# A CIN layer stack on one core: the shared terms V1 and V0 as matmuls of 32 by 64, with x loaded in halves for them

## The chip, the cores and the metric

The kernel runs on one core of a Trainium2 chip. The metric is the device time of one execution in microseconds (us), lower is better. The time before is 486.74 us, the median of 3 runs (486.42 to 490.46). All data is float32.

## What is computed

A compressed interaction network with three layers over x of shape (B = 1024, F = 64, E = 16), cut to what matters:

```python
for i in range(3):
    z = jnp.einsum('bfe,bge->bfge', x0, h).reshape(B, 64 * 64, 16)   # all products of x0 and h
    y = jnp.einsum('oc,bce->boe', Ws[i], z) + bs[i][None, :, None]   # 128 outputs
    x_i, h = (y[:, :64], y[:, 64:]) if i != 2 else (y, y)            # first half kept, second half goes on
    xs.append(x_i)
pooled = jnp.sum(jnp.concatenate(xs, axis=1), axis=2)
return pooled @ fc_w.T + fc_b
```

The result is one number for each of the 1024 rows. Because what is kept of a layer is only summed with the weights of `fc_w`, the kept half of layer 0 is a quadratic form of x (its 64x64 matrix is called V0 here), the kept half of layer 1 is x times V1 times h1, and layer 2 is a quadratic form too, whose matrix (V2, W2 weighed with `fc_w`) is folded into weights called Q. Only the half of layer 0 that goes on, h1, needs all 64 outputs.

## The kernel before, in words

The host sorts x into 32 chunks of 32 rows: a chunk is 64 features by N = 512 columns (32 rows times E). For each chunk the kernel loads `xa` (128 partitions x 4 x 512, x shifted by 0 to 3 features) and `xb` (128 x 4 x 512, x shifted by more), 1 MB each, from SP's queue (`load_xa`, `load_xb`, lines 131 to 148). `xra` holds 132 rows of 512 for each chunk, and the first 64 of them are x itself.

Work for one chunk:

- `product` (line 219): VectorE multiplies `xa` by `xb` for j = 0 to 3, 128 x 2048 each, into tiles `z` (12 buffers). After the last one ScalarE writes a 32-row square into z (line 228).
- `contract` (line 256): 16 matmuls of 128x128 by 512 columns for each chunk, accumulated in PSUM (`acc`): one half of the rows is h1, the other half is Q's part (which half depends on whether the chunk is odd).
- `contract_shared` (line 265), once for four chunks: V1 times x is added to the Q half (line 274), V0 times x goes to tiles `ys` (line 278), and the squares of x's first 32 features times `w_sq` are added to `acc` (line 284). For V1 and V0 two chunks stand above each other in a tile `xx` (128 x 512), and each matmul takes 64 rows and 64 columns of the array. The weights are `v1w` and the diagonal blocks of `bd`. For the squares four chunks stand in one tile `sq`, 32 rows each, and each matmul takes 32 rows and 64 columns.
- `squares` (line 230) and `last_tile` (line 236): ScalarE makes `sq` from `xa` (32 rows at a time, line 234) and copies x from `xa` into `xx` (64 rows at a time, line 243).
- `factors` (line 324): ScalarE copies the Q half out (line 330), and VectorE adds the bias to h1 and multiplies the two (line 336). `x_v0x` (line 340): VectorE multiplies `ys` by `xx`. `sums` (line 343): VectorE sums over E.

Stages. A head (to some 43 us) loads weights and four chunks (2, 3, 0, 1), computes h1 for them with matmuls of 128x64 by 256 (line 296), makes V2 and from it Q (through a DRAM tile `md` and back, lines 450 to 533), and then adds Q's part for chunks 0 and 1 (`head_q`, line 310, matmuls of 128x64 by 512). Then the main loop goes through the chunks in the order 4, 5, 6, 7, 2 and 3 (head chunks), 8, 9, and so on to 31. Loads and products run ahead of the matmuls by two chunks, as buffers come free (3 buffers for `xa`, 3 for `xb`).

The order of work is written out by hand: each engine runs its instructions in the order of the program, and so does SP with the transfers that it issues. Ahead of the main loop the order on VectorE is: products of chunk 4; `w1x` is weighed with `fc_w` (`weigh`, lines 570 and 571) into `v1h`, which four copies of 64x32 put into `v1w` (line 582); products of chunk 5. Within the loop's first step: `w0x` is weighed, and four copies put `v0h` into `bd` (line 594); products of chunks 6 and 7. SP issues in the same order: chunk 4, `w1x`, chunk 5, `w0x`, chunk 6, chunk 7. `keep_clock` (line 103) lets TensorE run some matmuls with a cleared `bd` at the very start.

Of the kernel before, what the change touches and what calls it, by code (L numbers as in the profile page):

```python
# [33 lines left out]
F32 = mybir.dt.float32  # L37
AF = mybir.ActivationFunctionType
# [3 lines left out]
F = 64  # L42
E = 16
B = 1024
CB = 32
N = CB * E
# [5 lines left out]
XR = 128 + NI  # L52
# [3 lines left out]
KEPT = HEAD[-2:]  # L56
NV = 200
FIRST = 4
# [4 lines left out]
def cin_kernel(ctx, tc, xra, xrb, wh, w0r, w1h, w2t, wx1, wx0, vec, out):  # L63
    nc = tc.nc
# [17 lines left out]
    def flat_tile(name):  # L82
        return z_tile(name).rearrange("p i n -> p (i n)")
# [11 lines left out]
    fv2 = const_tile("fv2", [128, 32])  # L95
    nc.scalar.copy(fv2, fc2.to_broadcast([128, 32]))

    bd = const_tile("bd", [128, 128])
    nc.gpsimd.memset(bd, 0.0)

    misc = ps.tile([128, N], F32, tag="acc", name="misc", bufs=4)

    def keep_clock(n):
        for _ in range(n):
            nc.tensor.matmul(misc[:, 0:128], bd, bd, start=True, stop=True)  # L105

    keep_clock(6)

    shift = const_tile("shift", [128, 96])
    nc.gpsimd.memset(shift, 0.0)  # L110
    for base in (0, 64, -64):
        nc.gpsimd.affine_select(
            out=shift, in_=shift, compare_op=ALU.not_equal, fill=1.0, base=base,
# [9 lines left out]

    w_all = const_tile("w_all", [128, NT, 192])
    w_sq = const_tile("w_sq", [128, 192])
    v1w = const_tile("v1w", [128, F])


    xas, xbs, xxs, sqs = {}, {}, {}, {}

    def load_xa(c, at=slice(0, NI)):
        if c not in xas or at.start == 0:
# [9 lines left out]
    def load_xb(c, first=NJ):  # L142

        xb = xp.tile([128, NJ, N], F32, tag="xb", name=f"xb_{c}")
        for at in (slice(0, first), slice(first, NJ)):
            if at.start < NJ:
                nc.sync.dma_start(out=xb[:, at, :], in_=xrb[c, :, at, :])
        xbs[c] = [xb[:, j, :] for j in range(NJ)]

    def load_chunk(c):  # L150
        load_xa(c)
        load_xb(c)

    c0, c1, c2, c3 = HEAD
# [51 lines left out]
    accs, uus, zs, ys, parts = {}, {}, {}, {}, {}  # L206
# [20 lines left out]
        if j == NJ - 1:  # L227
            nc.scalar.activation(zs[c, j][SQ, 0, :], xas[c][SQ, 0, :], AF.Square)  # L228

    def squares(c):  # L230
        if c // 4 not in sqs:
            sqs[c // 4] = xp.tile([128, N], F32, tag="zl", name=f"sq_{c}", bufs=3)
        at = slice(32 * (c % 4), 32 * (c % 4) + 32)
        nc.scalar.activation(sqs[c // 4][at], xas[c][0:32, 0, :], AF.Square)  # L234

    def last_tile(c):

        if c >= FIRST:
            squares(c)
        if c % 2 == 0:  # L240
            xxs[c // 2] = sp.tile([128, N], F32, tag="xx", name=f"xx_{c}", bufs=5)
        to = halves[c % 2]
        nc.scalar.copy(xxs[c // 2][to], xas[c][to, 0, :])  # L243

    def w_cols(c):
        return slice(64, 192) if c % 2 else slice(0, 128)

# [4 lines left out]
    def pieces(c):  # L252

        return parts[c] if c in parts else [(accs[c], slice(0, N))]
# [10 lines left out]
    def contract_shared(first):  # L265

        chunks = range(first, first + 4)
        ends = chunks if first == 0 else chunks[:2]
        for k in (first // 2, first // 2 + 1):
            ys[k] = ps.tile([128, N], F32, tag="y", name=f"y_{k}")  # L270
            for n in range(2):
                c, rows, q = 2 * k + n, halves[n], halves[1 - n]
                for acc_c, cols in pieces(c):
                    nc.tensor.matmul(  # L274
                        acc_c[q], v1w[rows], xxs[k][rows, cols], start=(c not in ends), stop=False,
                    )
            for rows in halves:
                nc.tensor.matmul(ys[k][rows], bd[rows, rows], xxs[k][rows], start=True, stop=True)  # L278
        for c in chunks:
            at = slice(32 * (c % 4), 32 * (c % 4) + 32)  # L280
            for acc_c, cols in pieces(c):
                for n in range(2):
                    h = n == c % 2
                    nc.tensor.matmul(  # L284
                        acc_c[halves[n]], w_sq[at, w_cols(c)][:, 64 * n : 64 * n + 64],
                        sqs[first // 4][at, cols], start=h and (first == 0 or c not in ends),
                        stop=(c in ends), tile_position=(at.start, 64 * n),
                    )

# [67 lines left out]


    new_acc(c0, H2)
    squares(c0)  # L360
    nc.scalar.copy(xb_gps[:, 0, :], xbs[c0][1])  # L361
    xbs[c0][1] = xb_gps[:, 0, :]
    product(c0, 1, engine=nc.gpsimd)
# [24 lines left out]
    new_acc(c1, H2)  # L388
    nc.scalar.copy(xb_gps[:, 1, :], xbs[c1][3])
    xbs[c1][3] = xb_gps[:, 1, :]  # L390
    squares(c1)

    product(c0, 3)
    load_chunk(c3)
# [9 lines left out]


    v2r = flat_tile("v2r")[:, 0:1024].rearrange("p (n c) -> p n c", n=2)
    v2t = const_tile("v2t", [128, F])
# [12 lines left out]
    for h in range(2):  # L420
        at = slice(32 * h, 32 * h + 32)
# [38 lines left out]
    for half, queue in enumerate((nc.sync, nc.scalar)):  # L460
        queue.dma_start(
            out=m_ap(0, 32 * half, [[row, F], [1, 32 * F]]), in_=m_rows[halves[half]]
# [5 lines left out]
        out=m_ap(64, 68, [[row, 4], [4 * F, 7], [1, 4 * F]]),  # L468
        in_=m_rows[0:4, 4 * F :].rearrange("p (k c) -> p k c", c=4 * F),
# [2 lines left out]
    keep_h1(c1)  # L472


    squares(c2)
    new_acc(c2, H2)
    for j in (0, 1):
        xb3 = ps.tile([128, N], F32, tag="y", name=f"xp_{c3}_{j}")
# [38 lines left out]
    product(c3, NJ - 1, engine=nc.gpsimd)  # L517
    for j in range(NJ - 1):
        product(c3, j)
    squares(c3)  # L520
# [6 lines left out]
    dg = const_tile("dg", [128, F])  # L527
    nc.sync.dma_start(out=dg[SQ], in_=m_ap(32, 32, [[row + F, 32], [1, F]]))
    nc.sync.dma_start(out=w_sq[:, 64:128], in_=m_ap(0, 0, [[0, 4], [row + F, 32], [1, F]]))

# [2 lines left out]
        nc.vector.tensor_tensor(w_all[:, at, 64:128], ms[:, 0, at], ms[:, 1, at], ALU.add)  # L533

    keep_h1(c3)
    for c in KEPT:
        last_tile(c)


    for j in range(NJ):  # L540
# [15 lines left out]
    def load_products(c, other=None):  # L556

        for n in (c,) if other is None else (c, other):
            if n not in made:
                load_chunk(n)  # L560
                last_tile(n)
                made.add(n)
        for j in range(NJ):
            product(c, j)

    def weigh(w, fc, out):
# [3 lines left out]
        nc.vector.tensor_tensor(w, w, fc.unsqueeze(1).to_broadcast([128, nk, n]), ALU.mult)  # L570
        nc.vector.tensor_reduce(out, w, AX.X, ALU.add)

    load_products(FIRST)


    w1x = set_tile("w1x")
    nc.sync.dma_start(out=w1x, in_=wx1)
    v1h = const_tile("v1h", [128, 32])
    weigh(w1x, fcr[:, 64:128], v1h)
    for to in halves:  # L580
        for n in range(2):
            nc.vector.tensor_copy(v1w[to, 32 * n : 32 * n + 32], v1h[halves[n]])

    load_products(FIRST + 1)

    def v0_weights():
        w0x = flat_tile("w0x")
        nc.sync.dma_start(out=w0x, in_=wx0)
        v0h = const_tile("v0h", [128, 32])
        weigh(w0x, fcr[:, 0:64], v0h)  # L590
        for to in halves:
            for n in range(2):
                cols = slice(to.start + 32 * n, to.start + 32 * n + 32)
                nc.vector.tensor_copy(bd[to, cols], v0h[halves[n]])


    NP = NCH // 2
    QP = NP // 4
    res = const_tile("res", [128, QP, CB])
    outs = out.rearrange("(k h b) o -> h k (b o)", h=2, b=CB)  # L600

    def pool(k0, k1, part=0, **flags):
# [16 lines left out]
    for s, c in enumerate(order):  # L619
        k, head = c // 2, c in HEAD  # L620
        if order[s - 1] in HEAD and not head:
            for n in range(NF // 2):
                x_v0x(n)
            for n in HEAD:
                factors(n)
                if n % 2:
                    sums(n // 2)
        if 0 < s < len(order) - 2 and s not in (2, 3):
            load_products(*order[s + 2 : s + (4 if s == 6 else 3)])
        if s in (2, 3):  # L630

            if s == 2:
                for n in order[4:6]:
                    load_chunk(n)
                    last_tile(n)
            for j in (0, 1) if s == 2 else (2, 3):
                for n in order[4:6]:
                    product(n, j)
        if not head:
            if c % 4 < 2:  # L640
                new_acc(c)
            for j in range(NJ):
                contract(c, j)
        elif c % 2:
            for n in (c - 1, c):
                new_acc(n)
            for j in range(NJ):
                head_q(k, j)
            contract_shared(0)
        if c % 4 == 1 and not head:  # L650
            for n in (1, 2):
                new_acc(c + n)
            contract_shared(c - 1)
        if s == 0:
            v0_weights()
            load_products(order[2], order[3])

        if c == HEAD[0] or c % 4 in (0, 3) and s and order[s - 1] not in HEAD:
            factors(order[s - 1])
            if order[s - 1] % 2:  # L660
                sums(order[s - 1] // 2)
        elif c % 4 == 2 and not head:
            factors(c - 2)
            factors(c - 1)
            x_v0x(k - 1)
            x_v0x(k)
            sums(k - 1)
# [94 lines left out]
```

## Time and profile before

| what | value |
|---|---|
| median of 3 runs | 486.74 us |
| profiled execution, its own time | 486.68 us |
| its span in the profile | 484.9 us |
| TensorE matmul (PE) busy | 479.8 us, 99% |
| VectorE (DVE) busy | 370.4 us, 76% |
| ScalarE (ACT) busy | 93.8 us, 19% |
| contract, line 260 | 928 matmuls, 387.3 us |
| V1, line 274; V0, line 278 | 66 and 64 matmuls, 15.5 us each (side by side) |
| squares, line 284 | 132 matmuls, 8.9 us |
| ScalarE: sq, line 234; xx, line 243 | 32 of 628 ns; 32 of 613 ns |
| DMA | 78.59 MB, mean 162 GB/s |

How to read it: in a row of groups stand the line, the engine, the operation, the tiles written and read, the shape, the count, the busy time and the mean of one. A float32 matmul of the program is two matmul instructions in the profile, so 66 stands for 33. "64*64" is rows by columns of the array that a matmul takes. Matmuls are pipelined, so the time between two starts tells the pace, and the length of one does not. A timeline row is: start, length, engine, line, operation, and in brackets the idle time before it and what ended it. PE is TensorE's matmuls, PEld its weight loads, POOL is GpSimd, SP the engine that issues most transfers; "DMA share" is the busy share of the core's 16 DMA engines.

### The profile page before, as it was taken

The numbers are of one execution on the slowest core, as the hardware profiler recorded it, in microseconds if no ns is written. First come the engines' busy times: TensorE is split into PE (matmuls) and PEld (weight loads), VectorE is DVE, ScalarE is ACT, GpSimd is POOL, SyncE is SP. The second block draws the span as 40 slices with busy tenths as digits, with TensorE's granted clock in tenths as the row PEclk, the third lists the DMA queues.
The fourth block names the chain that finished last, engine by engine and source line by source line (L and its number), as shares of the span: only waits on it lengthen the run. The fifth ranks groups of instructions, "written<-read, shape, count | busy, mean of one in ns | idle before, by whom it ended". The sixth has DMA issues, their size and how long they took to land.

```text
span 484.9 us, 4057 instructions
## 1 busy us (share of the span) xinstructions
PE 479.8 (99%) x1672; PEld 215.7 (44%) x1672; DVE 370.4 (76%) x234; ACT 93.8 (19%) x165; POOL 17.3 (4%) x15
## 2 busy tenths in 40 slices
PE   9999999999999999999999999999999999999996
PEld 4564344443344344444444344443444434444465
DVE  5984799998899988898887686767878676771312
ACT  4244012021212030312221012212022121020001
POOL 5350000000000000000000000000000000000000
PEclk9999999999999999999999999999999999999999
DMA  8986984441743453547343344433344430000000
GB/s 334 412 266 181 427 349 174 173 173 64 307 182 142 173 207 140 194 174 279 113 187 120 148 174 173 161 128 105 126 173 173 170 145 32 0 1 0 0 2 0
DMA packets 14392, 78.59 MB, mean 162 GB/s; under 512 B 3778, under 2 KB 4450, under 8 KB 5478
## 3 DMA queue, kind: packets, MB, share of 16 engines
q1 hardware_dynamic: 13266, 77.05, 41.4%
q10 hardware_dynamic: 1108, 1.28, 1.0%
q8 instruction: 13, 0.21, 0.2%
q14 instruction: 5, 0.04, 0.0%
HBM read 76.69 MB, written 1.64 MB: 162 GB/s over the span
## 4 chain that ended last, share of the span: by engine, by line
PE 97%; DVE 1%; ACT 1%; SPq 1%; issue 1%; DMA 0%; POOL 0%; DVEq 0%; POOLq 0%
PE acc L260 80%; PE acc L314 6%; PE acc L296 4%; PE acc L274 3%; PE acc L284 2%; PE xp L184 1%; PE misc L105 1%; SPq L465 0%; DVE z L223 0%; ACT m_sb L445 0%; PE pv L411 0%; DMA md<-m_sb 0%; PE pm L435 0%; PE y L278 0%; PE po L604 0%
## 5 line engine op out<-in xcount | busy, mean ns | idle before, releaser
L260 PE MATMUL acc<-z,w_all 128*128 128x512 f32 (+1 forms) x928 | 387.3, 578 | 0.0
L223 DVE TENSOR_TENSOR z<-xa,xb 128x2048 f32<-128x2048 f32 x125 | 280.7, 2286 | 41.4 <-PE acc L260 34.8
L260 PEld LDWEIGHTS acc<-z,w_all 128*128 128x128 f32 x928 | 175.5, 190 | 211.3 <-issue 205.8
L228 ACT ACTIVATE z<-xa 32x512 f32<-32x512 f32 x34 | 21.3, 626 | 322.7 <-DVE z L223 318.1
L336 DVE SCALAR_TENSOR_TENSOR uu<-acc,vs,q 64x512 f32<-64x512 f32 (+1 forms) x29 | 21.2, 731 | 57.7 <-ACT q L330 57.5
L296 PE MATMUL acc<-z,w_all 128*64 128x256 f32 x256 | 28.9, 381 | 0.2 <-DVE z L223 0.2
L314 PE MATMUL acc<-z,w_all 128*64 128x512 f32 x128 | 27.9, 593 | 0.0
L330 ACT COPY q<-acc 64x512 f32<-64x512 f32 (+1 forms) x33 | 18.7, 567 | 37.4 <-PE acc L260 21.2
L223 DVE TENSOR_TENSOR z<-xa,xp 128x2048 f32<-128x2048 f32 (+2 forms) x10 | 18.1, 1856 | 7.2 <-PE xp L184 6.0
L296 PEld LDWEIGHTS acc<-z,w_all 128*64 128x64 f32 x256 | 18.0, 137 | 11.0 <-issue 1.3
L234 ACT ACTIVATE sq<-xa 32x512 f32<-32x512 f32 x32 | 20.1, 628 | 3.4 <-DMA xa<-in_xra 2.7
L345 DVE TENSOR_REDUCE acc<-uu 128x64 f32<-128x1024 f32 (+3 forms) x19 | 20.3, 1073 | 0.3
L243 ACT COPY xx<-xa 64x512 f32<-64x512 f32 x32 | 19.6, 613 | 0.3
L314 PEld LDWEIGHTS acc<-z,w_all 128*64 128x64 f32 x128 | 9.1, 137 | 18.0 <-issue 17.9
L278 PE MATMUL y<-xx,bd 64*64 64x512 f32 x64 | 15.5, 603 | 0.0
L274 PE MATMUL acc<-xx,v1w 64*64 64x512 f32 (+1 forms) x66 | 15.5, 588 | 0.0
L341 DVE SCALAR_TENSOR_TENSOR uu<-y,cx,xx 128x512 f32<-128x512 f32 x16 | 11.3, 746 | 0.2
L223 POOL TENSOR_TENSOR z<-xa,xb_gps 128x2048 f32<-128x2048 f32 x2 | 9.1, 4568 | 4.7 <-ACT xb_gps L361 4.4
L284 PE MATMUL acc<-sq,w_sq 32*64 32x512 f32 (+1 forms) x132 | 8.9, 599 | 0.0
L274 PEld LDWEIGHTS acc<-xx,v1w 64*64 64x64 f32 x66 | 4.1, 132 | 10.6 <-issue 10.3
L223 POOL TENSOR_TENSOR z<-xa,xb 128x2048 f32<-128x2048 f32 x1 | 6.6, 6570 | 13.3 <-DVE z L223 13.3
L184 PE MATMUL xp<-xa,shift 64*64 64x512 f32 x32 | 5.5, 786 | 0.1
(57 smaller groups left out, 60.0 us busy)
## 6 DMA issues: line engine op xcount, KB each, us to landing
xa<-in_xra SPq DMA_DIRECT2D x32, 1024.0 KB, 5.0
xb<-in_xrb SPq DMA_DIRECT2D x31, 1024.0 KB, 7.1
w<-in_w2t SPq DMA_DIRECT2D x2, 1024.0 KB, 10.9
xa<-in_xra SPq DMA_DIRECT2D x2, 768.0 KB, 7.9
w1s<-in_w1h SPq DMA_DIRECT2D x1, 1024.0 KB
w1x<-in_wx SPq DMA_DIRECT2D x1, 1024.0 KB
w0x<-in_wx SPq DMA_DIRECT2D x1, 1024.0 KB, 8.3
w0t<-in_w0r SPq DMA_DIRECT2D x1, 768.0 KB
```

The lines of the kernel that those rows point to most:

```text
L223: engine.tensor_tensor(zs[c, j][:, at, :], xas[c][:, at, :], xbs[c][j].unsqueeze(1).to_broadcast([128, last - first, N]), ALU.mult,)
L228: nc.scalar.activation(zs[c, j][SQ, 0, :], xas[c][SQ, 0, :], AF.Square)
L234: nc.scalar.activation(sqs[c // 4][at], xas[c][0:32, 0, :], AF.Square)
L243: nc.scalar.copy(xxs[c // 2][to], xas[c][to, 0, :])
L260: nc.tensor.matmul(acc_c, w_all[:, t, w_cols(c)], zs[c, j][:, i, cols], start=(t == 0 and c % 4 < 2), stop=(t == NT - NI and c % 4 >= 2),)
L274: nc.tensor.matmul(acc_c[q], v1w[rows], xxs[k][rows, cols], start=(c not in ends), stop=False,)
L284: nc.tensor.matmul(acc_c[halves[n]], w_sq[at, w_cols(c)][:, 64 * n : 64 * n + 64], sqs[first // 4][at, cols], start=h and (first == 0 or c ...
L296: nc.tensor.matmul(accs[c][halves[n]], w_all[:, t, 0:64], zs[c, j][:, i, n * H2 : (n + 1) * H2], start=(t == 0), stop=(j == last and i == ...
L314: nc.tensor.matmul(accs[c][halves[1 - c % 2]], w_all[:, t, 64:128], zs[c, j][:, i, :], start=(t == 0), stop=False,)
L330: nc.scalar.copy(q[h, cols], acc_c[64 - h.start : 128 - h.start])
L336: nc.vector.scalar_tensor_tensor(uu[:, cols], acc_c[h], bh1[h], q[h, cols], ALU.add, ALU.mult)
L345: nc.vector.tensor_reduce(acc[rows, of, k, half], uus[k][rows, of, E * half.start : E * half.stop].rearrange("p k (b e) -> p k b e", e=E), ...
```

## The change

- V1 and V0 become matmuls of 32 rows by 64 columns, in the shape that the squares have. Each of the four chunks of a group has a row group of 32 of its own, and its 64 features come as two halves of 32 that are accumulated (m = 0, 1). For each half the order is chunk by chunk, V1 then V0. The squares follow as before.
- The weights become `v1w` and `v0w`, 128 x 2 x 64: in each row group of 32 both halves of the weights. `to_groups` writes each with 16 copies of 32x32 on VectorE, where there were four of 64x32.
- `load_shared`, new, once for four chunks: SP loads a tile `xr` (128 x 2 x 512: four chunks times 32 features, two halves) with two transfers, and two tiles `xx` (two chunks times 64 features) with one transfer each, all straight from `xra`, 256 KB each. One ScalarE square of 128 x 512 makes `sq`. It is called after the loads of the first chunk of a group (chunks 4, 8, 12, ...), and for group 0 after the loads of chunks 2 and 3 in the main loop.
- `squares` and `last_tile`, and so ScalarE's 32-row squares and 64-row copies, are gone.
- Buffers: `xr` 2, `sq` 2, `xx` 4 in place of 5. `v2t` and `dg` now lie in the tile `res`, `v1h` and `v0h` in `shift`, and `v0w` takes the place of the cleared `bd` for `keep_clock`.

```diff
+    v0w = const_tile("v0w", [128, 2, F])
+    v1w = const_tile("v1w", [128, 2, F])
+    zeros = v0w.rearrange("p h g -> p (h g)")
+    nc.gpsimd.memset(zeros, 0.0)
...
+    def load_shared(first):
+
+        xr = xrs[first] = sp.tile([128, 2, N], F32, tag="xr", name=f"xr_{first}")
+        for h in range(2):
+            nc.sync.dma_start(
+                out=xr[:, h, :],
+                in_=bass.AP(
+                    tensor=xra.tensor, offset=(first * XR + 32 * h) * N,
+                    ap=[[XR * N, 4], [N, 32], [1, N]],
+                ),
+            )
+        for k in (first // 2, first // 2 + 1):
+            xxs[k] = sp.tile([128, N], F32, tag="xx", name=f"xx_{k}", bufs=4)
+            nc.sync.dma_start(
+                out=xxs[k],
+                in_=bass.AP(
+                    tensor=xra.tensor, offset=2 * k * XR * N, ap=[[XR * N, 2], [N, F], [1, N]]
+                ),
+            )
+        sqs[first] = sp.tile([128, N], F32, tag="sq", name=f"sq_{first}")
+        nc.scalar.activation(sqs[first], xr[:, 0, :], AF.Square)
...
-            for n in range(2):
-                c, rows, q = 2 * k + n, halves[n], halves[1 - n]
+        groups = {c: slice(32 * (c % 4), 32 * (c % 4) + 32) for c in chunks}
+        for m in range(2):
+            for c, at in groups.items():
+                n, xr = c % 2, xrs[first][groups[c], m]
                 for acc_c, cols in pieces(c):
                     nc.tensor.matmul(
-                        acc_c[q], v1w[rows], xxs[k][rows, cols], start=(c not in ends), stop=False,
+                        acc_c[halves[1 - n]], v1w[at, m], xr[:, cols],
+                        start=(m == 0 and c not in ends), stop=False,
+                        tile_position=(at.start, 64 * (1 - n)),
                     )
-            for rows in halves:
-                nc.tensor.matmul(ys[k][rows], bd[rows, rows], xxs[k][rows], start=True, stop=True)
+                nc.tensor.matmul(
+                    ys[c // 2][halves[n]], v0w[at, m], xr, start=(m == 0), stop=(m == 1),
+                    tile_position=(at.start, 64 * n),
+                )
...
                 load_chunk(n)
-                last_tile(n)
+                if n % 4 == 0:
+                    load_shared(n)
...
+    def to_groups(w, part):
+
+        for at in range(0, 128, 32):
+            for n in range(2):
+                for m in range(2):
+                    q = 64 * n + 32 * m
+                    nc.vector.tensor_copy(
+                        w[at : at + 32, m, 32 * n : 32 * n + 32], part[q : q + 32]
+                    )
...
-    for to in halves:
-        for n in range(2):
-            nc.vector.tensor_copy(v1w[to, 32 * n : 32 * n + 32], v1h[halves[n]])
+    to_groups(v1w, v1h)
...
             if s == 2:
                 for n in order[4:6]:
                     load_chunk(n)
-                    last_tile(n)
+                load_shared(0)
```

More of the change, by code (lines that the diff above doesn't have):

```diff
@@ L96, in cin_kernel @@
     nc.scalar.copy(fv2, fc2.to_broadcast([128, 32]))
-    bd = const_tile("bd", [128, 128])
-    nc.gpsimd.memset(bd, 0.0)
+    v0w = const_tile("v0w", [128, 2, F])
+    v1w = const_tile("v1w", [128, 2, F])
+    zeros = v0w.rearrange("p h g -> p (h g)")
+    nc.gpsimd.memset(zeros, 0.0)
     misc = ps.tile([128, N], F32, tag="acc", name="misc", bufs=4)
@@ L104, in keep_clock @@
         for _ in range(n):
-            nc.tensor.matmul(misc[:, 0:128], bd, bd, start=True, stop=True)
+            nc.tensor.matmul(misc[:, 0:128], zeros, zeros, start=True, stop=True)
     keep_clock(6)
@@ L125, in cin_kernel @@
     w_sq = const_tile("w_sq", [128, 192])
-    v1w = const_tile("v1w", [128, F])
-    xas, xbs, xxs, sqs = {}, {}, {}, {}
+    res = const_tile("res", [128, 128])
+    xas, xbs, xxs, xrs, sqs = {}, {}, {}, {}, {}
     def load_xa(c, at=slice(0, NI)):
@@ L228, in product @@
             nc.scalar.activation(zs[c, j][SQ, 0, :], xas[c][SQ, 0, :], AF.Square)
[L230 to L243, printed above, removed]
     def w_cols(c):
@@ L270, in contract_shared @@
             ys[k] = ps.tile([128, N], F32, tag="y", name=f"y_{k}")
-            for n in range(2):
-                c, rows, q = 2 * k + n, halves[n], halves[1 - n]
+        groups = {c: slice(32 * (c % 4), 32 * (c % 4) + 32) for c in chunks}
+        for m in range(2):
+            for c, at in groups.items():
+                n, xr = c % 2, xrs[first][groups[c], m]
                 for acc_c, cols in pieces(c):
                     nc.tensor.matmul(
-                        acc_c[q], v1w[rows], xxs[k][rows, cols], start=(c not in ends), stop=False,
-                    )
-            for rows in halves:
-                nc.tensor.matmul(ys[k][rows], bd[rows, rows], xxs[k][rows], start=True, stop=True)
-        for c in chunks:
-            at = slice(32 * (c % 4), 32 * (c % 4) + 32)
+                        acc_c[halves[1 - n]], v1w[at, m], xr[:, cols],
+                        start=(m == 0 and c not in ends), stop=False,
+                        tile_position=(at.start, 64 * (1 - n)),
+                    )
+                nc.tensor.matmul(
+                    ys[c // 2][halves[n]], v0w[at, m], xr, start=(m == 0), stop=(m == 1),
+                    tile_position=(at.start, 64 * n),
+                )
+        for c, at in groups.items():
             for acc_c, cols in pieces(c):
@@ L285, in contract_shared @@
                         acc_c[halves[n]], w_sq[at, w_cols(c)][:, 64 * n : 64 * n + 64],
-                        sqs[first // 4][at, cols], start=h and (first == 0 or c not in ends),
+                        sqs[first][at, cols], start=h and (first == 0 or c not in ends),
                         stop=(c in ends), tile_position=(at.start, 64 * n),
@@ L359, in cin_kernel @@
     new_acc(c0, H2)
-    squares(c0)
     nc.scalar.copy(xb_gps[:, 0, :], xbs[c0][1])
@@ L390, in cin_kernel @@
     xbs[c1][3] = xb_gps[:, 1, :]
-    squares(c1)
     product(c0, 3)
@@ L406, in cin_kernel @@
     v2r = flat_tile("v2r")[:, 0:1024].rearrange("p (n c) -> p n c", n=2)
-    v2t = const_tile("v2t", [128, F])
+    v2t = res[:, 0:F]
     for n in range(2):
@@ L472, in cin_kernel @@
     keep_h1(c1)
-    squares(c2)
     new_acc(c2, H2)
@@ L519, in cin_kernel @@
         product(c3, j)
-    squares(c3)
     keep_h1(c2)
@@ L526, in cin_kernel @@
             read_columns(j, nc.scalar if half and j == 2 else nc.sync, half)
-    dg = const_tile("dg", [128, F])
+    dg = res[:, F:128]
     nc.sync.dma_start(out=dg[SQ], in_=m_ap(32, 32, [[row + F, 32], [1, F]]))
@@ L535, in cin_kernel @@
     keep_h1(c3)
-    for c in KEPT:
-        last_tile(c)
     for j in range(NJ):
@@ L577, in cin_kernel @@
     nc.sync.dma_start(out=w1x, in_=wx1)
-    v1h = const_tile("v1h", [128, 32])
+    v1h = shift[:, 0:32]
     weigh(w1x, fcr[:, 64:128], v1h)
-    for to in halves:
-        for n in range(2):
-            nc.vector.tensor_copy(v1w[to, 32 * n : 32 * n + 32], v1h[halves[n]])
+    to_groups(v1w, v1h)
     load_products(FIRST + 1)
@@ L588, in v0_weights @@
         nc.sync.dma_start(out=w0x, in_=wx0)
-        v0h = const_tile("v0h", [128, 32])
+        v0h = shift[:, 32:64]
         weigh(w0x, fcr[:, 0:64], v0h)
[L591 to L594, printed above, removed]
+        to_groups(v0w, v0h)
     NP = NCH // 2
     QP = NP // 4
-    res = const_tile("res", [128, QP, CB])
+    res = res.rearrange("p (k b) -> p k b", b=CB)
     outs = out.rearrange("(k h b) o -> h k (b o)", h=2, b=CB)
```

## The prediction

> **What bounds the kernel now.** I read the page first: its shares by engine, its forty slices, its chain. Then the timeline of TensorE, the timeline of VectorE between 50 and 85 us, and the table of stretches for DMA.
>
> ```profile
> PE 479.8 (99%) x1672; PEld 215.7 (44%) x1672; DVE 370.4 (76%) x234; ACT 93.8 (19%) x165; POOL 17.3 (4%) x15
> ...
> PE   9999999999999999999999999999999999999996
> ...
> DVE  5984799998899988898887686767878676771312
> ...
> DMA  8986984441743453547343344433344430000000
> ...
> PE 97%; DVE 1%; ACT 1%; SPq 1%; issue 1%; DMA 0%; POOL 0%; DVEq 0%; POOLq 0%
> ```
>
> TensorE is the bound: 97% of the chain. So an edit is worth what it takes from TensorE's stream, or what it makes TensorE wait. DVE and DMA are nearly full only in the first third, where a delay could reach TensorE.
>
> ```profile
> 159.19 0.65 PE L274 MATMUL acc<-xx,v1w 64*64 64x512 f32 x2
> 159.21 0.65 PE L278 MATMUL y<-xx,bd 64*64 64x512 f32 x2
> 159.67 0.59 PE L274 MATMUL acc<-xx,v1w 64*64 64x512 f32 x2
> ...
> 160.10 0.60 PE L274 MATMUL acc<-xx,v1w 64*64 64x512 f32 x2
> ...
> 160.53 0.60 PE L274 MATMUL acc<-xx,v1w 64*64 64x512 f32 x2
> ...
> 161.07 1.11 PE L284 MATMUL acc<-sq,w_sq 32*64 32x512 f32 x16
> 162.12 55.20 PE L260 MATMUL acc<-z,w_all 128*128 128x512 f32 x128
> ```
>
> A program matmul is two of these in f32. The starts show rounds: four 64*64 matmuls together, a new four each 0.43 us, four rounds for V1 and V0; then the sixteen 32*64 squares in two rounds of eight. One group of four chunks takes 162.12 - 159.19 = 2.93 us. The last V round starts at 160.53 and the squares 0.54 later, not 0.43: the change of shape costs 0.11. The first round of a shape takes 0.48, 0.05 over the rest.
>
> ```profile
> 51.76 8.90 DVE L223 TENSOR_TENSOR z<-xa,xb 128x2048 f32<-128x2048 f32 x4 [6.08 <-DMA xb<-in_xrb]
> 60.57 2.28 DVE L570 TENSOR_TENSOR w1x<-w1x,vs 128x2048 f32<-128x2048 f32 x1
> 62.89 2.29 DVE L571 TENSOR_REDUCE v1h<-w1x 128x32 f32<-128x2048 f32 x1
> 65.21 0.74 DVE L582 COPY v1w<-v1h 64x32 f32<-64x32 f32 x4
> 65.98 8.90 DVE L223 TENSOR_TENSOR z<-xa,xb 128x2048 f32<-128x2048 f32 x4
> 74.80 2.29 DVE L570 TENSOR_TENSOR w0x<-w0x,vs 128x2048 f32<-128x2048 f32 x1
> ...
> 79.44 0.76 DVE L594 COPY bd<-v0h 64x32 f32<-64x32 f32 x4
> ```
>
> This is the tightest place. VectorE waits for chunk 4's x until 51.76, then works without a gap: chunk 4's products, w1x weighed, chunk 5's products (the first done at 65.98 + 2.2 = 68.2), w0x weighed. TensorE starts chunk 5 at 70.3 (chunk 4 at 56.47, 32 matmuls of 0.43). The slack is 2.1 us.
>
> ```profile
> 45.20:45.55 0.35, 0.35 (x4) 0.14 (x2) 0.14 (x2) 0.35 (x1) 0.00 (x0) 1.00 0.28 65
> 46.40:48.10 1.70, 1.70 (x10) 0.57 (x8) 0.00 (x0) 0.04 (x1) 0.00 (x0) 1.00 0.99 410
> ```
>
> The last two columns are the busy share of the 16 DMA engines and GB/s. In the first stretch only w_sq (line 529) moves, a source whose outermost dimension is 4 into 128 partitions: share 0.28, some four engines. In the second, chunk 4 (outermost dimension 128) moves: 0.99.
>
> **The change, part by part.**
>
> *V1 and V0 as 32 by 64.* 16 program matmuls for a group in place of 8, eight tiles at a time in place of four: again four rounds. Squares: two rounds, as now. Six rounds without a change of shape save 0.11 + 0.05 = 0.16 us a group, 8 groups: 1.3 us. Bounds: the squares' own pace is 1.05/2 = 0.52 a round with both edges, so six rounds are at most 3.1, which would cost 0.2 a group, 1.6 in all; I take -1.3, since eight tiles started 7 ns apart fit in the 0.43 round.
>
> *ScalarE.* Out go 32 squares (0.628) and 32 copies (0.613), 39.7 us; in come 8 squares of 128x512 of about 0.6, 5 us. ScalarE is 19% busy and mostly waits for products, so nearly nothing. One exception: at 31.73 a square stood ahead of the copies that released the products before line 296, where TensorE idled 0.16; I take -0.1. Each new square waits for xr; behind it stands the square of its chunk's last product, 6 us later for chunk 4, so it hides.
>
> *POOL and the shared tiles.* POOL clears v0w in place of bd, the same 128x128 (0.2 us). v2t, dg, v1h and v0h move into tiles (res, shift) whose other readers are done or far off: no wait.
>
> *VectorE.* 16 copies of 32x32 in place of 4 of 64x32, twice. A copy has a pitch of 0.77/4 = 0.19, set by its start and not by rows (32x64 at line 542: 0.19). So 12 x 0.19 = 2.3 us more ahead of chunk 5's first product, and again ahead of V0. By itself this ends the slack: 68.2 + 2.3 = 70.5 against 70.3, 0.2 of wait, and v0w ready at 80.2 + 4.6 = 84.8 against 84.2, some 0.4 more. Both vanish under what follows.
>
> *DMA: the step that decides.* SP issues four more transfers for a group, and for the first group they stand between chunk 4 and w1x, chunk 5, w0x. They add 1 MB: two for xr (source 4 by 32 rows of 2 KB), two for xx (2 by 64 rows). Like w_sq, their source begins with a small dimension. By that row, xr runs on 4 engines and xx, which no row shows, on 2; its bounds are one engine and sixteen. The trace's 2,048-byte packets took 84 ns. On the busiest engines that is 2 x 32 x 84 ns = 5.4 us for xr and 2 x 64 x 84 ns = 10.8 us for xx: 16.1 us. On all sixteen it would be 2.7 in all, and hidden.
>
> SP's issue itself is about 0.6 us each (w_sq's was 0.60), 2.4 us ahead of w1x, hidden: the engines are busy with chunk 4 until 51.4. From the third group on, xr waits for TensorE and xx for VectorE to release the tiles of two groups before; the next chunk's loads queue behind, but their own tiles come free later still (98.6 against 118.1 at chunks 8 and 9), so this is nothing.
>
> SP's transfers are served in order: chunk 4 (2 MB) came by 51.7, which is 2 MB at 410 GB/s after 46.4, with w1x and chunk 5 issued before 47.1. So every engine ends chunk 4 near 51.4; the busiest end xr and xx at 67.5 and their part of w1x (1 MB / 410 GB/s = 2.5) at 70.0. VectorE, in order, starts line 570 at 70.1 in place of 60.57. Weighing takes 65.21 - 60.57 = 4.64, to 74.7; the copies 16 x 0.19 = 3.1, to 77.8 (chunk 5 lands near 75); the first product 2.3, to 80.1. TensorE has been idle since 70.3: 9.8 us. Whether all four use the same engines no row tells: if they do not overlap, the longest lane is 5.4, w1x lands before 60.6, and nothing waits.
>
> The Trainium skill, "DMA: Bandwidth & Descriptors", section "Why a DMA increments its semaphore by 16 and not by 1", says that a hardware queue uses the largest number of engines up to 16 that divides the slowest dimension on both sides, and always the lowest-numbered ones. That speaks against this change: 4 and 2, on the same engines, so 9.8 us; the row alone leaves anything from 0 to 9.8.
>
> *The clock after the wait.* TensorE's first matmuls of the kernel run at half pace: the rounds at line 184 start 0.85 apart until 6.6 us, from 1.0, so 5.6 us at half, 2.8 us lost. At the end the granted clock reads 0.50 at 484.6, 2.1 us after the last matmul. A wait of 9.8 should bring the same: bounds 0 and 2.8, and I take 2.8, the only row of a restart.
>
> The skill's "TensorE: Matmul & The Clock Gate", Part 1, puts the fall at one idle window of 3.4 us and the return after one busy window; an estimate from it is 1.7 to 3.4 us lost. With its ends the sum below would be 496.7 to 498.4.
>
> *What is late next.* VectorE resumes 14 us late, TensorE 12. V0's weights are ready at 77.8 + 8.8 + 4.6 + 3.1 = 94.3; TensorE comes to them at 80.1 + 13.8 + 2.8 = 96.7. Chunk 6's first product had 4.6 us of slack (82.5 against 87.1) and keeps 3. The next group's xr and xx delay chunk 9 by some 4 us for VectorE, which had 9. After 170 us VectorE needs about 43 us a group against TensorE's 58, and a lane carries 36: no more waits.
>
> **The sum**, against the profiled execution's 486.68 (span 484.9 and 1.8 around it; the median of the runs is 486.74, the same): 486.7 + 9.8 + 2.8 - 1.3 - 0.1 = 497.9.
>
> **The rivals.**
>
> *The lanes don't collide* (sixteen engines, or other engines for each transfer). The saved switches less 0.6 of VectorE's copies: 486.7 - 1.4 + 0.6 = 485.9, not slower. For it: no row shows a leading 2 or two such transfers at once. Against it: w_sq's 0.28. It decides when the busiest engine's extra is under 60.5 - 51.4 - 2.5 = 6.6 us and the 2.1 of slack is left for the copies.
>
> *Half a collision*: xx on four engines too. Lane 10.8, wait 9.8 - 5.4 = 4.4, clock 0 to 2.8: 489.7 to 492.5.
>
> *TensorE pays itself*: tiles of one row group in turn, eight V rounds in place of four: 4 x 0.43 x 8 = 13.8 us: 499.7 without the DMA wait, 511.7 with it. Against it: the sixteen squares, two tiles to each row group, need 1.05 us, not 1.7.
>
> **How the numbers follow.** Forecast 0.75; half a collision 0.08; no collision 0.15; TensorE pays 0.02. The forecast's own bounds are 495.1 (no clock loss) to about 501 (3 us more for slower rows or a second wait at chunk 10). To leave out no more than 2 in 10 the range goes down through half a collision: 490 to 501. Changes within 1% (4.9 us) are about what a measurement here cannot tell from none. Slower by over 1%: 0.75 + 0.02 + half of 0.08 = 0.81. Within: 0.15 less 0.01, and 0.04: 0.18. Faster: 0.01.
>
> **What would show it.** In the profile after: a stretch from 55 to 67 us with a DMA share of 0.12 to 0.25; line 570's part waiting for w1x some 9 us on VectorE; TensorE idle near 70 to 80 with a product as releaser, and matmuls of twice the length after it; xx landing in 5 us or more when alone; groups of V and squares in 2.77 us in place of 2.93. I am wrong if the DMA share stays near 1 until w1x has landed, or if VectorE starts it before 62.

## The result, and the profile after

The changed kernel takes 502.84 us, the median of 6 runs (502.31 to 503.13), beside 486.72 us for 6 runs of the kernel before: a ratio of 1.0304 (95% interval 1.0264 to 1.0343), so it is slower by 3%. The profiled execution took 502.96 us with a span of 500.8, 15.9 more than the span before.

The page of the kernel after, its busy times, slices and chain:

```profile
PE 481.7 (96%) x1802; PEld 218.6 (44%) x1802; DVE 373.7 (75%) x258; ACT 59.7 (12%) x109; POOL 17.3 (3%) x15
...
PE   9999954999999989999999999999999999999996
...
DVE  5992729999883999888897987786877778681311
...
PEclk9999995999999999999999999999999999999999
DMA  8977496445368428545645671564444533000000
...
PE 83%; DMA 7%; DVE 6%; SPq 2%; issue 1%; ACT 1%; DVEq 0%
...
L272 PE MATMUL acc<-z,w_all 128*128 128x512 f32 (+1 forms) x928 | 390.7, 582 | 14.0 <-DVE z L250 14.0
```

TensorE's busy time hardly moved, but it is no longer full: slices 6 and 7 (63 to 88 us) are at 5 and 4 tenths, slice 7 at half the clock, and 14.0 us of idle time stand before line 272 (`contract`), where there were 0.0, with a product of VectorE as releaser. The chain, 97% TensorE before, now runs through DMA (7%) and VectorE (6%).

VectorE's timeline after, the part that answers to the one shown before:

```profile
52.16 8.90 DVE L250 TENSOR_TENSOR z<-xa,xb 128x2048 f32<-128x2048 f32 x4 [6.36 <-DMA xb<-in_xrb]
72.17 2.29 DVE L582 TENSOR_TENSOR w1x<-w1x,vs 128x2048 f32<-128x2048 f32 x1 [11.12 <-DMA w1x<-in_wx]
74.50 2.29 DVE L583 TENSOR_REDUCE shift<-w1x 128x32 f32<-128x2048 f32 x1
76.82 2.96 DVE L591 COPY v1w<-shift 32x32 f32<-32x32 f32 x16
79.81 8.90 DVE L250 TENSOR_TENSOR z<-xa,xb 128x2048 f32<-128x2048 f32 x4
...
93.27 3.03 DVE L591 COPY v0w<-shift 32x32 f32<-32x32 f32 x16
```

Chunk 4 arrives as before (52.16 against 51.76). Then VectorE stands for 11.1 us until `w1x` is there, weighs it, makes 16 copies where there were 4, and only then multiplies chunk 5.

TensorE's timeline after, from chunk 4 to chunk 10 (line 272 is `contract`; line 288 opens the first group of V and squares):

```profile
55.97 14.00 PE L272 MATMUL acc<-z,w_all 128*128 128x512 f32 x32
82.16 16.96 PE L272 MATMUL acc<-z,w_all 128*128 128x512 f32 x32 [12.19 <-DVE z L250]
99.05 0.64 PE L288 MATMUL acc<-xr,v1w 32*64 32x512 f32 x1
...
101.81 27.73 PE L272 MATMUL acc<-z,w_all 128*128 128x512 f32 x64
...
146.12 14.00 PE L272 MATMUL acc<-z,w_all 128*128 128x512 f32 x32
160.42 13.97 PE L272 MATMUL acc<-z,w_all 128*128 128x512 f32 x32 [0.30 <-DVE z L250]
...
178.71 4.56 PE L272 MATMUL acc<-z,w_all 128*128 128x512 f32 x10 [1.56 <-DVE z L250]
```

From start to start chunk 4 took 13.84 us before; now it is 82.16 - 55.97 = 26.19. Chunk 5 itself is 3 us longer than chunk 4. The group of V and squares takes 101.81 - 99.05 = 2.76. Chunks 9 and 10 wait once more, a little.

The table of stretches after (PE, PEld, DVE, ACT, POOL, then the clock, the DMA share and GB/s):

```profile
46.40:48.10 1.70, 1.70 (x10) 0.57 (x8) 0.00 (x0) 0.00 (x0) 0.00 (x0) 1.00 0.94 376
...
53.50:56.00 2.50, 2.50 (x13) 0.61 (x9) 2.50 (x2) 0.63 (x1) 0.00 (x0) 1.00 0.26 102
57.00:59.00 2.00, 2.00 (x6) 0.89 (x5) 2.00 (x2) 0.00 (x0) 0.00 (x0) 1.00 0.16 56
...
63.00:65.00 2.00, 2.00 (x6) 0.89 (x5) 0.00 (x0) 0.00 (x0) 0.00 (x0) 1.00 1.08 321
...
70.00:72.00 2.00, 0.00 (x0) 0.00 (x0) 0.00 (x0) 0.00 (x0) 0.00 (x0) 1.00 1.00 422
...
76.00:78.00 2.00, 0.00 (x0) 0.00 (x0) 1.89 (x8) 0.00 (x0) 0.00 (x0) 0.50 1.02 430
```

Four stages show. While `xr` moves alone, the share is 0.26 (4 engines of 16). While `xx` moves alone it is 0.16, and 0.13 in the second half of that stretch (2 engines of 16). From 61 to 69 `w1x` and chunk 5 move beside the rest of `xx`: every engine is busy, but at 291 to 321 GB/s. From 70, with `xx` done, the same share gives 422 to 430.

The ledger, from the starts of TensorE's calls in both traces:

| place | us |
|---|---|
| head, to chunk 4 (56.47 to 55.97) | -0.5 |
| wait before chunk 5 (13.84 to 26.19) | +12.35 |
| chunk 5 at half clock (13.83 to 16.89) | +3.06 |
| chunks 9 and 10 late | +2.2 |
| V and squares, 2.93 to 2.76, 7 groups | -1.1 |
| sum; the spans differ by 15.9 | +16.0 |

### The profile page after: what moved, and what is told of

It is laid out like the page before. It is cut to its first block, busy times and chain, and to the rows that moved or that the text cites. A ratio compares the mean times of both kernels' runs of the same rounds, so it can differ in the third digit from the quotient of the medians.

```text
span 500.8 us, 4361 instructions
## 1 busy us (share of the span) xinstructions
PE 481.7 (96%) x1802; PEld 218.6 (44%) x1802; DVE 373.7 (75%) x258; ACT 59.7 (12%) x109; POOL 17.3 (3%) x15
## 3 DMA queue, kind: packets, MB, share of 16 engines
HBM read 85.08 MB, written 1.64 MB: 173 GB/s over the span
## 4 chain that ended last, share of the span: by engine, by line
PE 83%; DMA 7%; DVE 6%; SPq 2%; issue 1%; ACT 1%; DVEq 0%
PE acc L272 72%; DMA w1x<-in_wx 4%; DVE z L250 3%; PE acc L331 3%; PE acc L288 2%; PE acc L313 2%; DMA xb<-in_xrb 1%; PE acc L301 1%; DMA md<-m_sb 1%; SPq L511 1%; PE xp L211 1%; DMA xa<-in_xra 1%; DVE uu L351 1%; DVE hb L350 1%; DVE v1w L591 1%
## 5 line engine op out<-in xcount | busy, mean ns | idle before, releaser
L293 PE MATMUL y<-xr,v0w 32*64 32x512 f32 x128 | 15.9, 600 | 0.0
L288 PE MATMUL acc<-xr,v1w 32*64 32x512 f32 (+1 forms) x132 | 15.7, 586 | 0.0
L582 DVE TENSOR_TENSOR w1x<-w1x,vs 128x2048 f32<-128x2048 f32 x1 | 2.3, 2291 | 11.1 <-DMA w1x<-in_wx 11.1
L288 PEld LDWEIGHTS acc<-xr,v1w 32*64 32x64 f32 x132 | 5.1, 131 | 9.9 <-issue 9.6
L175 ACT ACTIVATE sq<-xr 128x512 f32<-128x512 f32 x8 | 5.0, 630 | 13.0 <-DMA xr<-in_xra 12.9
```

The source lines that it names most:

```text
L288: nc.tensor.matmul(acc_c[halves[1 - n]], v1w[at, m], xr[:, cols], start=(m == 0 and c not in ends), stop=False, tile_position=(at.start, 6 ...
L293: nc.tensor.matmul(ys[c // 2][halves[n]], v0w[at, m], xr, start=(m == 0), stop=(m == 1), tile_position=(at.start, 64 * n),)
```

## The experiments

Theory A: the transfers' form costs the time, because a source that begins with 4 or 2 keeps each on few engines and `w1x` stands behind them. Theory B: the added megabyte for each group costs it, in whatever form. Theory C: the matmuls of 32 by 64 or VectorE's 16 copies cost it.

### The same bytes on all engines

```diff
-        for h in range(2):
+        for n in range(4):
...
-                out=xr[:, h, :],
+                out=xr[32 * n : 32 * n + 32],
...
-                    ap=[[XR * N, 4], [N, 32], [1, N]],
+                    ap=[[N, 32], [32 * N, 2], [1, N]],
...
-                out=xxs[k],
+                    out=xxs[k][halves[n]],
...
-                    ap=[[XR * N, 2], [N, F], [1, N]]
+                    ap=[[N, F], [1, N]]
```

> The changed kernel, with the same bytes of xr and xx loaded by eight transfers for a group in place of four: one for each chunk's xr (32 rows outermost) and one for each chunk's xx (64 rows outermost), none with a source that begins with 4 or 2. Theory A (few engines: a transfer whose source begins with a small dimension runs on that many engines, and what stands behind it in SP's queue waits for them): the waits near 60 and near 150 us vanish, w1x lands by 57, and the time is 486 (485 to 487.5), the saved changes of shape less some waits for VectorE's copies. Theory B (the amount: 1 MB more and more transfers ahead of w1x hold it up, whatever their form): 500 or more, since there are now eight transfers. Theory C (the 32 by 64 matmuls and the sixteen copies cost the time): unchanged, 503.

Measured: 486.42 us (12 runs, 485.62 to 489.8), ratio to before 0.9993 (0.9968 to 1.0017). In its trace `w1x` makes nobody wait, and chunk 5 waits 0.57. VectorE's timeline of this kernel:

```profile
60.91 2.29 DVE L583 TENSOR_TENSOR w1x<-w1x,vs 128x2048 f32<-128x2048 f32 x1
63.23 2.29 DVE L584 TENSOR_REDUCE shift<-w1x 128x32 f32<-128x2048 f32 x1
65.55 2.96 DVE L592 COPY v1w<-shift 32x32 f32<-32x32 f32 x16
68.54 8.90 DVE L251 TENSOR_TENSOR z<-xa,xb 128x2048 f32<-128x2048 f32 x4
```

With that, four transfers for `xr` and two for each `xx`, the whole loss goes: it hangs on the form of the transfers. B and C fall: bytes, matmul shape and copies are all still in this kernel. The form changes three things together: how many engines carry a transfer, how many transfers there are, and how many partitions each one writes (32 or 64 in place of 128).

### Before, with the four transfers added and not read

```diff
+                if n % 4 == 0:
+                    load_more(n)
```

`load_more` issues the four transfers of the change into tiles that nothing reads.

> The kernel before, with the changed kernel's four transfers for a group added at the same places in SP's queue, into tiles that nothing reads; V1, V0 and the squares stay as they were. (sq has 2 buffers and xx 4 in place of 3 and 5, and some small tiles share space, as in the changed kernel, to make room.) Theory A: the wait for w1x comes without any other part of the change, 11 us on VectorE, and the time is 501 to 504. Theory B: the same. Theory C: 487.

Measured: 498.62 us (one run). `w1x` came at 72.62 and chunk 5 waited 6.9. In this one execution the head ended 3.2 us later (chunk 4 at 59.63), which gave VectorE that much more time, and its 4 copies in place of 16 gave 2.2 more; so the size is under the expectation. The transfers alone, in the old kernel, bring the wait.

> As the kernel before with the unread transfers added, but these in the eight-transfer form with 32 and 64 rows outermost. Theory A: 487, within 1 us of before: 1 MB more for a group on all engines takes 2.7 us and hides. Theory B: as with the four transfers, 500 or more.

Measured, the same unread transfers in the wide form: 486.59 us (one run), span 484.8. One megabyte more for each group costs nothing when all engines carry it.

### One kind of transfer narrow, the other wide

> The changed kernel with only xr left in its two transfers (source outermost 4), and each xx loaded by two transfers of 64 rows. If the busiest lanes add up (xr 2 x 32 packets of 84 ns = 5.4 us on four engines, xx 1.4 on all): w1x lands at 51.5 + 5.4 + 1.4 + 2.5 = 60.8, just when VectorE wants it, TensorE waits 1 us at chunk 5 at most, and the time is 486.5 to 488.5. If any transfer on few engines, or the number of transfers, does the harm: 495 or more.

Measured, `xr` narrow and `xx` wide: 493.55 us, ratio 1.0116 (0.9986 to 1.0247, two runs). The interval takes in 1, so what this kernel shows is in its trace. The time lies between the two expectations and the working was a miss: `w1x` came at 65.69, not 60.8, and chunk 5 waited 5.9. The table of stretches of this kernel:

```profile
52.00:54.00 2.00, 2.00 (x12) 0.71 (x10) 2.00 (x1) 0.00 (x0) 0.00 (x0) 1.00 1.09 212
54.00:57.00 3.00, 3.00 (x13) 1.01 (x10) 3.00 (x3) 0.63 (x1) 0.00 (x0) 1.00 1.05 238
57.00:60.00 3.00, 3.00 (x9) 1.33 (x8) 3.00 (x2) 0.00 (x0) 0.00 (x0) 1.00 1.01 228
...
63.00:66.00 3.00, 3.00 (x9) 1.32 (x8) 0.31 (x1) 0.00 (x0) 0.00 (x0) 1.00 1.03 434
```

With narrow transfers beside wide ones every engine is busy and about half as much moves: 228 to 238 GB/s from 54 to 60, then 434. (From 52 to 54 the rows of the wide `xx` are still among them.) My expectation counted only the time of the narrow lanes.

> The other half: xr by four transfers of 32 rows, each xx in its one transfer (source outermost 2). If the lanes add up: xx holds two engines for 10.8 us and longer where w1x's packets run beside it (its packets took 115 ns there in the changed kernel), w1x lands near 68, TensorE waits some 7.5 us at chunk 5 and 2.8 for the clock, and 2 to 4 at chunks 9 and 10: 496 to 500. If xr's form were the cause: 487.

Measured, `xx` narrow and `xr` wide: 496.2 us, ratio 1.0171 (1.0041 to 1.03, two runs), within its 496 to 500. `w1x` at 68.84, chunk 5 waits 9.0 and runs 2.45 longer. Either kind alone is enough for a wait, and `xx` on 2 engines weighs more in these two traces.

### Place of the narrow transfers

```diff
+        if first == FIRST:
+            for n in range(4):
...
+        else:
             for h in range(2):
```

The first group's transfers are wide, those of the others as in the change.

> The changed kernel, with only the first group's (chunks 4 to 7) xr and xx in the eight-transfer form; the other seven groups keep the four. Theory A: the wait for w1x, the wait of TensorE at 70 and the half clock after it vanish (12.4 + 3.1 = 15.5), and the later narrow transfers find some 15 us more of slack than VectorE left them, so the second wait (2.2) goes too: 485.5 to 488. If the later groups hurt by themselves: up to 490. Theory C: 503.

Measured: 495.49 us (one run), a miss. The head of this execution was 3.3 late, and later groups cost 4.8: chunk 9 waited 3.15 and chunk 10 1.64. TensorE's timeline of this kernel:

```profile
135.74 14.00 PE L291 MATMUL acc<-z,w_all 128*128 128x512 f32 x32
152.73 13.97 PE L291 MATMUL acc<-z,w_all 128*128 128x512 f32 x32 [3.00 <-DVE z L269]
...
171.03 1.55 PE L291 MATMUL acc<-z,w_all 128*128 128x512 f32 x3 [1.56 <-DVE z L269]
```

So the second place is a loss of its own, which the first wait covers in part: TensorE comes there 10 us earlier in this kernel than in the change.

```diff
-                if n % 4 == 0:
+                if n % 4 == 0 and n != FIRST:
                     load_shared(n)
+                if n == FIRST + 2:
+                    load_shared(FIRST)
```

> The changed kernel, with the first group's four transfers issued behind chunk 6's loads in place of behind chunk 4's; their form and the other groups stay. Theory A: w1x, chunk 5, w0x and chunk 6 are no longer behind them, so the wait of 12.4 and the half clock go, and what is left is the later groups' own wait at chunks 9 and 10, which was 4.8 us when only the first group was wide (there TensorE came 15 us sooner than in the changed kernel, so it waited more): 489.5 to 492. If the form costs wherever it stands: 500 or more.

Measured: 491.51 us, ratio 1.007 (1.0028 to 1.0111), within its 489.5 to 492. The same narrow transfers, issued after chunk 6's loads: chunk 5 starts at 70.30 without a wait. What is left is at chunk 9:

```profile
131.23 14.00 PE L272 MATMUL acc<-z,w_all 128*128 128x512 f32 x32
148.65 16.75 PE L272 MATMUL acc<-z,w_all 128*128 128x512 f32 x32 [3.42 <-DVE z L250]
```

```diff
-            nc.sync.dma_start(
+            nc.scalar.dma_start(
```

This is done for all four transfers of `load_shared`.

> The changed kernel, with the four transfers of every group issued from ScalarE's queue in place of SP's; the same packets on the same few engines. If the harm is the order within one queue (what SP issues later stands behind them, and SP's own issue stalls): w1x no longer waits for them, lands before 62, and the time is 486.5 to 491, the rest being ScalarE's own stalls of some 8 us a group while it issues. If the harm is the work on the busiest engines, whoever issues it: w1x lands near 70 again and the time is 498 or more.

Measured: 495.52 us, ratio 1.0157 (1.0027 to 1.0287, two runs), between both expectations. `w1x` makes no wait any more: it was there by 65.60, at least 6.5 us sooner than in the change, so the order in one queue was how it came to be late. But out of SP's order `xr` moved beside chunk 4's own load, which then landed at 56.78 in place of 52.16. TensorE's timeline of this kernel:

```profile
59.22 30.58 PE L272 MATMUL acc<-z,w_all 128*128 128x512 f32 x64 [3.08 <-DVE z L250]
```

TensorE waited 3.08 us ahead of chunk 4, and its granted clock stood at 0.50 from 58.2 to 65.0. Chunk 5 follows chunk 4 without a wait, but the two together take 2.85 us longer than before. Three later waits of 0.75 to 1.45 us came to it. The collision moved, it did not go.

### Few engines or short rows?

```diff
-                    ap=[[XR * N, 4], [N, 32], [1, N]],
+                    ap=[[XR * N, 4], [4 * N, 8], [1, 4 * N]],
-                    ap=[[XR * N, 2], [N, F], [1, N]]
+                    ap=[[XR * N, 2], [4 * N, 16], [1, 4 * N]],
```

The diff is against the unread transfers above. Their tile is another too: each transfer writes 32 partitions of 8 KB, in place of 128 partitions of 2 KB.

> The kernel before, with four unread transfers of 256 KB for each group again on 4, 4, 2 and 2 engines, but with rows of 8 KB in place of 2 KB (the same bytes on the same engines). It tells whether wide loads that run beside few-engine transfers are slowed by the few engines or by the short rows. With 2 KB rows the wide loads moved 293 to 328 GB/s between 62 and 70 us and VectorE got w1x 19.5 us after chunk 4 (53.1 to 72.6). If the few engines slow them: again 280 to 340 GB/s at a DMA share near 1 while a few-engine transfer is under way, w1x 19 to 20 us after chunk 4, and 496 to 501 us. If the short rows slow them: 400 to 430 GB/s there, the lanes at 309 ns a packet (16 x 309 ns on 4 engines, 32 x 309 ns on 2, 14.8 us in all) and w1x 2.5 us behind, 17 to 18 us after chunk 4, and 494 to 498 us. In both the few-engine transfers show shares of 0.25 and 0.13 while alone.

Measured: 516.1 us (one run), beyond both. The table of stretches and VectorE's timeline of this kernel:

```profile
58.00:60.00 2.00, 2.00 (x6) 0.95 (x5) 2.00 (x2) 0.00 (x0) 0.00 (x0) 1.00 1.05 242
...
66.00:68.00 2.00, 2.00 (x6) 0.88 (x5) 0.00 (x0) 0.00 (x0) 0.00 (x0) 1.00 1.04 238
...
78.00:80.00 2.00, 0.00 (x0) 0.00 (x0) 0.69 (x1) 0.00 (x0) 0.00 (x0) 0.50 1.02 410
```

```profile
51.31 8.89 DVE L244 TENSOR_TENSOR z<-xa,xb 128x2048 f32<-128x2048 f32 x4 [6.07 <-DMA xb<-in_xrb]
79.31 2.29 DVE L593 TENSOR_TENSOR w1x<-w1x,vs 128x2048 f32<-128x2048 f32 x1 [19.10 <-DMA w1x<-in_wx]
```

With rows of 8 KB the share stands near 1 from 54 to 76 us at some 205 to 250 GB/s, and packets of 8 KB take some 600 ns (median) in place of 309. `w1x` comes 28 us after chunk 4. So it does not take short rows to slow the wide loads. In this kernel SP's issues were short (1.3 to 1.4 us for two), so that wide and narrow transfers overlapped from the start; in the change SP was held, and they met only after 60.

### Half of the weight copies on ScalarE

```diff
-                    nc.vector.tensor_copy(
-                        w[at : at + 32, m, 32 * n : 32 * n + 32], part[q : q + 32]
-                    )
+                    copy = nc.scalar.copy if at >= 64 else nc.vector.tensor_copy
+                    copy(w[at : at + 32, m, 32 * n : 32 * n + 32], part[q : q + 32])
```

This stands on top of the wide form.

> The change with its transfers in the wide form (all 16 engines), and 8 of the 16 weight copies of each set on ScalarE in place of VectorE. In the wide form TensorE waited 0.57 us at chunk 5 because VectorE's 16 copies (2.96 us) stood ahead of its products. With 8 copies on VectorE (1.5 us) the first product of chunk 5 is ready at 65.55 + 1.5 + 2.3 = 69.3, ahead of 70.3, so that wait goes. If it is all the copies' time: 485.4 to 486.2 us, 0.6 under the wide form's 486.4 at most, which five rounds can hardly tell from no change. If ScalarE's copies of 32x32 come too late for V0 (over 0.25 us each), the wait moves to the shared group at 84.1 and nothing is gained.

Measured: 485.06 us (12 runs, 484.73 to 489.6), ratio to before 0.9971 (0.9947 to 0.9996), a little under its range. Chunk 5 follows chunk 4 at 13.84 with no wait, and the groups take 2.76. So the change with wide transfers and half of the copies moved is worth some 0.3%: of the 1.7 us between the profiled spans seven groups bring 1.1, and the rest is a head that ended earlier (chunk 4 at 55.92 against 56.47).

## Why the prediction was wrong, step by step

It had the sign and the place right, and the time, 502.84, lies above its 501.

*The shapes.* Right: 0.16 us a group was forecast and 2.93 became 2.76 or 2.77; seven groups gave 1.1, the last one nothing. *VectorE's copies*: 3.1 forecast, 2.96 and 3.03 measured. *ScalarE*: busy time fell from 93.8 to 59.7 us and brought at most the head's 0.5, which is not shown to be its doing: the wide form has the same work on ScalarE, and chunk 4 started there at 56.49, as before.

*How many engines.* Right: 4 and 2, by the shares 0.26 and 0.13. Here the rule of the Trainium skill ("DMA: Bandwidth & Descriptors", section "Why a DMA increments its semaphore by 16 and not by 1"), the largest divisor up to 16 of the slowest dimension on both sides, agrees with the trace, and it settled what the row of `w_sq` left open. These shares rule out half a collision (`xx` on four engines), and the groups' 2.76 us rules out that TensorE pays.

*How long the lanes are: the step that failed.* "The trace's 2,048-byte packets took 84 ns" was read at the start of the kernel before, where such rows went to 128 partitions on all engines. In the change it held only while the narrow transfers had the engines to themselves or nearly so: from 51 to 61 us. From 61, beside `w1x` and chunk 5, the packets of `xx` took 115 ns, and those of 8 KB 445 in place of 309. `xr` ended at 56.5 (forecast 56.8). At 84 ns `xx` would have ended at 67.3; by an estimate with its last 75 or so packets for an engine at 115 ns it ends at 69.6 (the last one did at 69.1), and `w1x`'s share (2.5) at 72.1: VectorE began at 72.17 where 70.1 was forecast. With TensorE 0.5 earlier, the wait was 12.35 in place of 9.8.

*SP's issue.* "Some 0.6 us each", hidden, failed too. SP's timeline after:

```profile
45.63 1.20 SPq L159 DMA_DIRECT2D xr<-in_xra  x2
46.87 7.04 SPq L168 DMA_DIRECT2D xx<-in_xra  x2
54.00 4.92 SPq L599 DMA_DIRECT2D w1x<-in_wx  x1
59.03 0.47 SPq L139 DMA_DIRECT2D xa<-in_xra  x1
```

SP was held 7.0 us at `xx` and 4.9 at `w1x`, so twelve to fourteen engines stood idle until about 59.5 instead of moving `w1x` and chunk 5, and the stretch of low share ended there and not at 67. In these runs the hold goes with the 2 KB rows, not with the few engines: in the wide form SP's four issues of `xx` took 5.4 us, and with rows of 8 KB on the same few engines two issues took 1.3 and `w1x` 0.36. The hold by itself was not what made `w1x` late: with rows of 8 KB SP issued it at 47.8, and VectorE had it only at 79.3. In the change the last of it had to go through the slow engines, where `xx` ended at 69.1.

*The clock.* 2.8 forecast, 3.06 measured, with the granted clock at 0.50 from 74.5 to 88.2. Elsewhere a loss of the clock cost less, 1.6 us at chunk 5 with the unread transfers. The length of the wait alone does not decide whether the clock falls: chunk 9 kept it after 3.00 us (first group wide: 14.0 us for the chunk), chunk 4 lost it after 3.08 (ScalarE's queue), and chunk 9 after 3.42 (issued later: 16.75). In the last two it fell 2.05 and 2.20 us into the wait. Within each trace the changes of the clock lie whole multiples of 3.41 us apart (it stayed at 0.50 for 6.8, 10.2, 13.7 or 17.1 us), so it also matters where a wait falls between these steps: the wait of 3.00 us lay across one, 1.3 us ahead of it and 1.7 behind. The Trainium skill ("TensorE: Matmul & The Clock Gate", Part 1) gives a free-running window of 3413 ns, and these steps agree with it. It lets the clock fall after at least one idle window of some 3.4 us, and that does not agree: here some 2.05 us of idle time were enough.

*What is late next: failed.* The delay of "some 4 us" at chunk 9, with 9 us to spare, and "no more waits" behind it overlooked that group 0's transfers and group 8's stand in SP's queue with chunk 8's loads alone between them, so two sets of lanes lie ahead of chunk 9. SP was held 12.13 us at group 8's `xx` and 5.21 at chunk 9's `xa`; VectorE stood idle 8.17 us for its `xb`, where no idle time was forecast, and TensorE lost 2.2 in all.

The terms that were off: 2.55 for the wait, 0.3 for the clock, 2.2 for the second wait, 0.2 for the last group, less 0.4 for the head: 4.8 of the 4.9 us by which the forecast was short. One slip of the sum had no effect: by its own terms the ends for the skill's clock are 496.8 and 498.5.

*The rival without a collision* is the wide form: 485.9 was worked out for it and 486.42 measured.

What stays open is why loads slow down on all engines at a share near 1. Short rows are not needed for it (8 KB rows on few engines slowed the rest more), and they are not enough: in the kernel before, from 5 to 7 us, rows of 2 KB into 128 partitions on all engines took 84 ns a packet at 373 to 422 GB/s. Few engines are not needed either: in the wide form the same rows into 32 and 64 partitions took 131 ns (median) at 255 GB/s from 52 to 54 us, with all engines busy. Nor is one queue: with ScalarE's, the total was 336 to 389 GB/s from 50 to 64 us, wide loads beside `xx`. What the slow cases share is that a transfer has fewer than 16 engines or writes fewer than 128 partitions. No run changes the partitions alone, so that is a candidate and not a cause.

## What to carry to other kernels

Read the outermost dimension of a transfer's source before its size: 256 KB whose source began with 2 cost more than 1 MB that began with 128, and the same bytes as transfers of 32 or 64 rows cost nothing. When a slow transfer stands in a queue ahead of something that is due, add the time for what overlaps it as well as its own lanes, and look at every place where two such transfers come close together. Here the engine that is the bound already ran at 99%, the new shape of its matmuls was worth 0.2 to 0.3%, and the loads that feed it decided the sign.

## What was not expected of the hardware

- A few engines' transfer slows the rest: beside wide loads the total fell from between 422 and 434 GB/s to 291 to 321 (2 engines, 2 KB rows), 228 to 238 (4 engines, 2 KB rows) and 205 to 250 (4 and 2 engines, 8 KB rows), at a share near 1.
- The engine that issues is held: 7.0, 4.9 and 12.1 us at places where 2 KB rows were under way, for issues that took 0.3 to 0.6 elsewhere; with the wide form's 2 KB rows on all engines too (5.4 us for four).
- Rows of 2 KB on all 16 engines moved 255 GB/s into 32 and 64 partitions (52 to 54 us of the wide form, a median of 131 ns each) and 373 to 422 GB/s into 128 (5 to 7 us of the kernel before, 84 ns each).
- The clock can fall some 2 us into a wait (2.05 and 2.20) and can outlast one of 3.00; its changes lie multiples of 3.41 us apart.
